# Borders of a 3x3 convolution stage: first norm by channel slot, part of the last group's statistics on ScalarE, merge on GpSimd, and four products of the last 1x1 convolution placed ahead of its scale

## The chip, the cores and the metric

The kernel runs on one core of one Trainium2 chip. The metric is the device time of one execution in microseconds (us). The engines are TensorE (PE, with its weight loads PEld), VectorE (DVE), ScalarE (ACT), GpSimd (POOL) and SyncE (SP, which here only issues DMAs).

## The reference

Two bottleneck blocks run one after the other on x of shape 64 x 1024 x 14 x 14, all in float32. A batch norm takes mean and variance over all 64 images and all pixels of a channel, from the very tensor that it normalizes.

```python
def _bn(x, gamma, beta):
    mean = jnp.mean(x, axis=(0, 2, 3), keepdims=True)
    var = jnp.var(x, axis=(0, 2, 3), keepdims=True)
    return gamma * (x - mean) * jax.lax.rsqrt(var + EPS) + beta

def block(x, ...):                                   # twice, with its own weights
    out = relu(_bn(conv1x1(x, w1) + b1, g1, be1))    # 1024 -> 256
    out = relu(_bn(conv3x3(out, w2) + b2, g2, be2))  # 256 -> 256, padding 1
    out = _bn(conv1x1(out, w3) + b3, g3, be3)        # 256 -> 1024
    return relu(x + softplus(residual_scale) * out)
```

## The kernel before

The 256 middle channels lie on 128 partitions in two slots, s = 0 and 1; the 1024 outer channels lie in eight. The images are taken two at a time as 32 tiles of 392 pixels for the 1x1 convolutions, and eight at a time as eight groups of 1568 pixels for the 3x3 convolution. The middle tensor of all images stays on the chip in `y_all`.

The order of the stages is: conv1 of block 0 (lines 1187 to 1207); conv2 of block 0 (`conv2`, line 543); a Gram matrix of its output, from which the statistics of conv3 are computed without conv3 (`gram`, line 904, and `conv3_stats`, line 981); then conv3 and the residual of block 0 together with conv1 of block 1 (`fused`, line 1060); conv2 of block 1; the Gram matrix of block 1; conv3 and the residual of block 1 (`residual`, line 1017, for the first and last tile, and `final`, line 1034, for pairs of tiles between). Between conv1 and conv2, and between conv2 and the Gram matrix, a batch norm closes: nothing of the next stage can start before the last value of the one before has entered the statistics. `aggregate` (line 1106) joins the partial statistics of each slot, and `affine` (line 1113) makes scale and shift from them by a chain of small instructions, one of them a square root on ScalarE.

Conv2 works by transforms along rows and columns. For each group `combine` (line 576) makes three pairs of row combinations, (1, 2), (3, 4) and (5, 0), in tiles t1, t2, ra and rb, with `stt` (line 574, VectorE) and `last` (line 571, ScalarE, the last row alone). `ready` (line 581) adds sums, differences and column differences, and has the filters loaded by SP, first the part ua and then the part ub (line 609). `Products` then multiplies on TensorE: `columns` goes into the banks even and odd, `whole` into l and m, and `biased` (line 679) moves these from PSUM on ScalarE. For the very first item the matmuls in `columns` are sorted so that slot 0 comes first (line 720). `finish` (line 751) is a generator on VectorE that turns the products of a group back into rows of `y_grp`.

The norm of the first conv happens in place: for group 0 before the first item (lines 854 to 855 and the function that `combine` calls between the two slots, line 860), for each later group on ScalarE while the group before is worked on (`long_work`, line 863). Group 0 is normalized so: slot 0 by ScalarE, rows 0 to 7 of slot 1 by VectorE, and the rest of slot 1 by ScalarE.

The statistics of conv2's output come in three ways. Group 0: bn_stats on VectorE (`first_stats`; `stat`, line 758, in five parts). Groups 1 to 6: two ScalarE passes for each slot with an accumulator, of value and of square around group 0's mean (`moment`, line 833). Group 7: bn_stats on VectorE in five parts. `merge` (line 839) joins the moments with small VectorE instructions and `entry` (line 818) writes them as one more bn_stats record.

In block 1 the statistics of conv3 end with 48 one-column matmuls into the bank ax; two products of the first tile, `made`, are computed ahead of them, into the two cx banks. `affine` follows, and `residual` computes the other six products, each with its own bank, and adds them to x.

Each engine works through its own list in order. The order within a list is partly that of the code (matmuls, `act`, and others wrapped in `keep_in_program_order`) and is otherwise set by a scheduler when the kernel is built. SP issues its DMAs in order, and a load waits until its buffer is free.

Of the kernel before, what the change touches and what calls it, by code (L numbers as in the profile page):

```python
# [41 lines left out]
P = 128  # L42
# [28 lines left out]

PARTS = 5

# [18 lines left out]
def bottlenecks(ctx: ExitStack, tc: tile.TileContext, x, w1s, w2s, w3s, pars, out):  # L92
# [450 lines left out]
    def conv2(psum, pool, b, par, aff, stats):  # L543
# [12 lines left out]
        moments = small.tile([P, MS, 2, NG - 2], FP, tag="moments", name="moments")  # L556
# [19 lines left out]
        def combine(g, pair, between=None):  # L576
# [40 lines left out]
            if pair[0] == 1:  # L617
                t1, t2 = new("t"), new("t")
                slots = [both] if between is None else [slice(s, s + 1) for s in range(MS)]
                for part in slots:  # L620
                    if part.start:
                        between()
                    last(t1, g, 2, -3.0, part)
                    last(t2, g, 1, -3.0, part)
                    for s in range(part.start, part.stop):
                        stt(t1[:, s, :full], rows(g, s, 2, 0, full), -4.0, rows(g, s, 4, 0, full))
                        stt(t2[:, s, :full], rows(g, s, 1, 0, full), -4.0, rows(g, s, 3, 0, full))
                    nc.vector.tensor_add(ra[:, part], t1[:, part], t2[:, part])
# [26 lines left out]
        class Products:  # L655
# [50 lines left out]
            def columns(self, *qs):  # L706

                r = self.r
                if self.four:
                    parts = {ODD: [(0, WH, D3M1, r[:, :, :, WH:])], EVEN: [(0, WH, D0M2, r[:, :, :, :WH])]}  # L710
                else:
                    parts = {
                        ODD: [(0, WH, D1, r[:, :, :, WH:]), (0, WH - 1, D3, r[:, :, :, WH + 1 :])],
                        EVEN: [(0, WH, D2, r[:, :, :, :WH]), (1, WH, D0, r[:, :, :, : WH - 1])],
                    }
                steps = [(q, o, part, s) for q in qs for o in range(MS) for part in parts[q] for s in range(MS)]
                if self.first:


                    steps.sort(key=lambda step: step[3])  # L720
                opened = set()
                for q, o, (a, e, k, v), s in steps:
                    to = self.banks[q][:, o].rearrange("p (l c) -> p l c", c=WH)[:, :, a:e]
                    matmul(
                        to, self.filter(s, o, k), v[:, s], start=self.first and q not in opened, stop=True,
                        skip_group_check=True,
                    )
                    opened.add(q)
                if self.first:
                    self.later(0, self.sums, ALU.add)  # L730
# [20 lines left out]
        def finish():  # L751


            for g in range(NG):
# [3 lines left out]
                def stat(k, lines):  # L758
                    if to is not None:
                        for o in range(MS):  # L760
                            nc.vector.bn_stats(to[:, o, k, :], lines[:, o])
# [25 lines left out]
                stat(2, out_rows[2])  # L787

# [7 lines left out]
                if g == NG - 1:  # L796
                    merge()
# [20 lines left out]
        def entry(half, count, mean, var):  # L818

            to = stats[:, :, 0, 3 * half : 3 * half + 3]  # L820
            nc.vector.memset(to[:, :, 0], float(count))
            nc.vector.tensor_copy(to[:, :, 1], mean)
            nc.vector.tensor_scalar(to[:, :, 2], var, float(count), None, ALU.mult)

        def begin():
# [5 lines left out]
            entry(0, GPX, mv[:, :, 0], mv[:, :, 1])  # L831

        def moment(g, o, k):
            act(
                idle, y_all[:, o, g * GPX : (g + 1) * GPX], (AF.Identity, AF.Square)[k], bias=center[:, o : o + 1],
                accum_out=moments[:, o, k, g - 1 : g],
            )

        def merge():

            n = GPX * (NG - 2)
# [3 lines left out]
            nc.vector.tensor_scalar(m, m, 1.0 / n, None, ALU.mult)  # L845
            var = small.tile([P, MS], FP, tag="m12var", name="m12var")
            nc.vector.tensor_mul(var, m[:, :, 0], m[:, :, 0])
            nc.vector.tensor_sub(var, m[:, :, 1], var)
            nc.vector.tensor_sub(m[:, :, 0], m[:, :, 0], center)
            entry(1, n, m[:, :, 0], var)  # L850


        top = 8
        norm(0, y_grp[:, 0, 0], aff)
        norm_vector(1, y_grp[:, 1, 0, :top], aff)

        def items():
            for g, pair in pairs:
                first = (g, pair) == pairs[0]
                for item in combine(g, pair, partial(norm, 1, y_grp[:, 1, 0, top:], aff) if first else None):  # L860
                    yield item

        def long_work(g, k):
# [6 lines left out]
            if g > 1 and i < 4:  # L870
                moment(g - 1, i // 2, i % 2)
# [241 lines left out]
    def affine(mv, n, par, g, be, conv_bias=None):  # L1113
# [10 lines left out]

        nc.vector.tensor_mul(q, r, v)
        nc.vector.scalar_tensor_tensor(q, q, -0.5, r, ALU.mult, ALU.mult)
        nc.vector.scalar_tensor_tensor(r, q, 1.5, r, ALU.add, ALU.mult)
        scale, shift = tl("scale"), tl("shift")
        nc.vector.tensor_mul(scale, r, par[:, g : g + n])
# [79 lines left out]
    for b in range(2):  # L1209
# [4 lines left out]
        aff = affine(aggregate(stats1, T - 3 + b), MS, pb, G1, BE1)  # L1214
        stats2 = keep.tile([P, MS, 1 + PARTS, nc.vector.BN_STATS_DIM], FP, tag="stats2", name=f"stats2_{b}")
# [3 lines left out]
        with tc.tile_pool(name=f"last_{b}", bufs=1) as one, tc.tile_pool(  # L1219
# [6 lines left out]
            with ExitStack() as scope:  # L1226
# [4 lines left out]
                with tc.tile_pool(name=f"gram_{b}", bufs=1) as pool:  # L1231
# [22 lines left out]
                    conv3_stats(psum, pool, grams, w3, mv3, ("cy", "cp", "cy", "cp" if b else "cx"))  # L1254
                aff = affine(mv3, CS, pb, G3, BE3, conv_bias=B3)
# [50 lines left out]
```

## Time and profile before

| what | us |
|---|---|
| median of 3 runs | 2015.49 (2012.01 to 2016.28) |
| the profiled execution | 2014.53 |
| its span, first to last instruction | 2012.5 |
| conv1 of block 0 | 0 to 308 |
| conv2 of block 0, to the scale of its norm | 308 to 604 |
| Gram matrix and conv3 statistics, block 0 | 604 to 700 |
| conv3 of block 0 with conv1 of block 1 | 700 to 1300 |
| conv2 of block 1, to the scale of its norm | 1300 to 1597 |
| Gram matrix and conv3 statistics, block 1 | 1597 to 1693 |
| residual of block 1 | 1693 to 2012.5 |

Times are counted from the first instruction. In a timeline a line has the start, the length from the first start to the last end of the instructions merged in it, the engine, the source line, the operation, what it writes and reads, and the number of instructions; in square brackets stands how long the engine was idle before, and who released it. In the chain of waits a line has start, share of time in us, and what was running. L169 is the helper through which all matmuls go, L327 the one for most of ScalarE's work, L574 is `stt`. In the table by stretches of time the columns are the length, then the busy time of PE, PEld, DVE, ACT and POOL with instruction counts, then the granted TensorE clock, the busy share of the DMA engines and GB/s.

### The profile page before, as it was taken

The numbers are of one execution on the slowest core, as the hardware profiler recorded it, in microseconds if no ns is written. First come the engines' busy times: TensorE is split into PE (matmuls) and PEld (weight loads), VectorE is DVE, ScalarE is ACT, GpSimd is POOL, SyncE is SP. The second block draws the span as 40 slices with busy tenths as digits, with TensorE's granted clock in tenths as the row PEclk, the third lists the DMA queues.
The fourth block names the chain that finished last, engine by engine and source line by source line (L and its number), as shares of the span: only waits on it lengthen the run. The fifth ranks groups of instructions, "written<-read, shape, count | busy, mean of one in ns | idle before, by whom it ended". The sixth has DMA issues, their size and how long they took to land.

```text
span 2012.5 us, 27547 instructions
## 1 busy us (share of the span) xinstructions
PE 1947.0 (97%) x9560; PEld 1640.9 (82%) x9560; DVE 1586.7 (79%) x2844; ACT 941.2 (47%) x1915; POOL 617.1 (31%) x676
## 2 busy tenths in 40 slices
PE   8999999999987999999999999899999888999999
PEld 4555558999987889999999999899999876555554
DVE  5788758999986566777777677699999864899997
ACT  1222214466645055555555555445566521555555
POOL 0111101121213133333433333211221140666665
PEclk9999999999998999999999999999999898999999
DMA  7866625555546534444444444256656374699998
GB/s 269 291 249 246 250 97 171 185 190 188 190 133 181 201 128 161 186 168 176 177 163 190 161 178 175 104 172 191 195 181 196 98 200 177 256 324 333 339 337 297
DMA packets 176218, 407.63 MB, mean 203 GB/s; under 512 B 12368, under 2 KB 143504, under 8 KB 159568
## 3 DMA queue, kind: packets, MB, share of 16 engines
q1 hardware_dynamic: 162208, 330.44, 48.0%
q10 hardware_dynamic: 5328, 50.86, 6.1%
q0 software_dynamic: 8544, 24.59, 3.6%
q8 instruction: 75, 1.23, 0.2%
q14 instruction: 63, 0.52, 0.1%
HBM read 267.95 MB, written 115.87 MB: 191 GB/s over the span
## 4 chain that ended last, share of the span: by engine, by line
PE 80%; DVE 12%; DMA 5%; ACT 1%; issue 1%; POOL 1%; SPq 0%; DVEq 0%; ACTq 0%; POOLq 0%
PE ay L169 16%; PE cy L169 13%; PE cp L169 11%; PE ap L169 10%; PE even L169 6%; PE odd L169 6%; PE m L169 5%; PE ax L169 5%; PE l L169 4%; PE cx L169 4%; DMA x<-mid 3%; DVE x L453 2%; PE ps L169 1%; DMA out<-x 1%; DVE sums L589 1%
## 5 line engine op out<-in xcount | busy, mean ns | idle before, releaser
L327 ACT ACTIVATE cu<-cy,scale 128x196 f32<-128x196 f32 (+1 forms) x552 | 257.3, 475 | 296.9 <-PE cy L169 289.4
L592 POOL TENSOR_TENSOR diffs<-r 128x448 f32<-128x448 f32 (+1 forms) x80 | 112.3, 1415 | 509.2 <-DVE r L574 262.7
L327 ACT ACTIVATE x<-x,shift 128x392 f32<-128x392 f32 x368 | 211.7, 614 | 69.3 <-POOL x L479 53.1
L453 DVE SCALAR_TENSOR_TENSOR x<-cp,scale,x 128x196 f32<-128x196 f32 (+1 forms) x368 | 178.0, 484 | 83.1 <-PE cp L169 81.0
L169 PE MATMUL cy<-ct,ws 128*128 128x196 f32 (+1 forms) x736 | 221.7, 383 | 2.5 <-ACT cu L327 2.5
L474 POOL TENSOR_TENSOR x<-x,cu 128x196 f32<-128x196 f32 (+1 forms) x184 | 167.5, 910 | 170.8 <-ACT cu L327 170.5
L169 PE MATMUL ay<-at,ws 128*128 128x196 f32 (+1 forms) x752 | 209.3, 381 | 1.0 <-ACT au L327 1.0
L479 POOL TENSOR_TENSOR x<-x,cu 128x392 f32<-128x392 f32 x124 | 126.1, 1017 | 190.9 <-DVE x L453 186.2
L169 PEld LDWEIGHTS ay<-at,ws 128*128 128x128 f32 x752 | 136.3, 190 | 35.1 <-ACT au L327 1.9
L169 PEld LDWEIGHTS cy<-ct,ws 128*128 128x128 f32 x736 | 133.6, 190 | 36.9 <-ACT cu L327 3.8
L500 POOL TENSOR_TENSOR x<-x,cu 128x392 f32<-128x392 f32 x120 | 125.1, 1043 | 83.5 <-DVE x L453 78.1
L169 PE MATMUL m<-sums,ua 128*128 128x224 f32 (+1 forms) x752 | 145.5, 336 | 0.0
L169 PE MATMUL cp<-zt 128*128 128x257 f32 x392 | 122.5, 395 | 16.3 <-DVE zt L948 16.3
L169 PE MATMUL cx<-y,w 128*128 128x196 f32 (+1 forms) x412 | 129.7, 402 | 5.0 <-DVE x L1025 5.0
L169 PEld LDWEIGHTS m<-sums,ua 128*128 128x128 f32 x752 | 131.3, 189 | 0.2
L453 DVE SCALAR_TENSOR_TENSOR x<-cx,scale,x 128x196 f32<-128x196 f32 (+1 forms) x184 | 89.1, 484 | 51.1 <-PE cx L169 50.8
L169 PE MATMUL cy<-y,w 128*128 128x196 f32 (+1 forms) x404 | 125.3, 396 | 0.0
L169 PE MATMUL even<-v,ub 128*128 128x224 f32 (+1 forms) x640 | 123.8, 334 | 0.7 <-ACT even L686 0.7
L169 PE MATMUL odd<-v,ub 128*128 128x224 f32 (+1 forms) x640 | 123.8, 335 | 0.2
L169 PE MATMUL l<-diffs,ub 128*128 128x224 f32 (+1 forms) x640 | 122.0, 333 | 0.0
L327 ACT ACTIVATE au<-ay 128x196 f32<-128x196 f32 (+1 forms) x141 | 53.8, 381 | 139.7 <-PE ay L169 139.0
L169 PE MATMUL cp<-y,ws 128*128 128x196 f32 (+1 forms) x368 | 113.8, 391 | 3.3 <-DVE x L453 1.8
(211 smaller groups left out, 4340.5 us busy)
## 6 DMA issues: line engine op xcount, KB each, us to landing
x<-in_x SPq DMA_DIRECT2D x62, 1568.0 KB, 6.7
ub<-u SPq DMA_DIRECT2D x80, 768.0 KB, 4.8
x<-mid SPq DMA_DIRECT2D x32, 1568.0 KB, 9.9
mid<-x ACTq DMA_DIRECT2D x31, 1568.0 KB, 5.2
out<-x SPq DMA_DIRECT2D x124, 392.0 KB, 6.6
ua<-u SPq DMA_DIRECT2D x96, 256.0 KB, 3.1
ub<-u SPq DMA_DIRECT2D x16, 1024.0 KB, 6.4
u<-y POOLq DMA_DIRECT2D x40, 256.0 KB, 6.3
```

What stands on the lines that cost most here:

```text
L169: tc.keep_in_program_order(nc.tensor.matmul(*args, **kw))
L327: tc.keep_in_program_order(nc.scalar.activation(*args, **kw))
L453: nc.vector.scalar_tensor_tensor(v, bank, self.scale[:, o : o + 1], v, ALU.mult, ALU.add)
L474: nc.gpsimd.tensor_add(self.part(1, 1), self.part(1, 1), u3)
L479: nc.gpsimd.tensor_add(v, v, self.u12)
L500: nc.gpsimd.tensor_add(v, v, self.u12[:, i * self.n : (i + 1) * self.n])
L589: nc.vector.tensor_add(sums, r[:, :, :, WH:], r[:, :, :, :WH])
L592: nc.gpsimd.tensor_sub(diffs, r[:, :, :, :WH], r[:, :, :, WH:])
```

## The change

Four things are edited.

First, the start of conv2. Scale and shift are made slot by slot, slot 1 first (`affine_by_slot`). Group 0 is normalized slot by slot just ahead of its combination: rows 7 to 13 by ScalarE and rows 0 to 6 by VectorE, for each slot. The matmuls of the first item take slot 1 first.

Second, the end of conv2. Of the five parts of group 7's statistics, VectorE keeps parts 3, 4 and 0. Parts 1 and 2, six rows of 112 pixels for each slot, are taken by ScalarE as two moments for each slot. The small instructions of the merge, behind its two reductions, run on GpSimd.

Third, in `affine` the multiplication by gamma is moved into r, ahead of the last step, so that the last step writes the scale.

Fourth, in block 1 four more products of the first tile, o = 2 to 5, are computed behind the conv3 statistics and ahead of the affine, into the banks cy and cp. Six of eight are then made ahead.

```diff
+LAST_PARTS = 3, 4, 0
...
-        moments = small.tile([P, MS, 2, NG - 2], FP, tag="moments", name="moments")
+        moments = small.tile([P, MS, 2, NG - 1], FP, tag="moments", name="moments")
...
-        def combine(g, pair, between=None):
+        def combine(g, pair, before=None):
...
-                slots = [both] if between is None else [slice(s, s + 1) for s in range(MS)]
+                slots = [both] if before is None else [slice(s, s + 1) for s in reversed(range(MS))]
                 for part in slots:
-                    if part.start:
-                        between()
+                    if before is not None:
+                        before(part.start)
...
-                    steps.sort(key=lambda step: step[3])
+                    steps.sort(key=lambda step: -step[3])
...
                 def stat(k, lines):
-                    if to is not None:
+                    if to is first_stats or to is not None and k in LAST_PARTS:
                         for o in range(MS):
-                            nc.vector.bn_stats(to[:, o, k, :], lines[:, o])
+                            nc.vector.bn_stats(to[:, o, k if to is first_stats else LAST_PARTS.index(k), :], lines[:, o])
...
                 stat(2, out_rows[2])
+                if g == NG - 1:
+                    for o in range(MS):
+                        lines = y_grp[:, o, g, 1 : 1 + 4 * full].rearrange("p (r k) l -> p r k l", k=4)[:, :, :2]
+                        for k in range(2):
+                            moment(lines, idle[:, : 2 * full * LINE].rearrange("p (r k l) -> p r k l", k=2, l=LINE), o, k, g)
+                    merge()
...
                 stat(4, end)
-                if g == NG - 1:
-                    merge()
...
-        def entry(half, count, mean, var):
+        def entry(eng, half, count, mean, var):
 
             to = stats[:, :, 0, 3 * half : 3 * half + 3]
-            nc.vector.memset(to[:, :, 0], float(count))
-            nc.vector.tensor_copy(to[:, :, 1], mean)
-            nc.vector.tensor_scalar(to[:, :, 2], var, float(count), None, ALU.mult)
+            eng.memset(to[:, :, 0], float(count))
+            eng.tensor_copy(to[:, :, 1], mean)
+            eng.tensor_scalar(to[:, :, 2], var, float(count), None, ALU.mult)
...
         def merge():
 
-            n = GPX * (NG - 2)
+            n = GPX * (NG - 2) + 2 * full * LINE
             m = small.tile([P, MS, 2], FP, tag="m12", name="m12")
             for o in range(MS):
                 nc.vector.tensor_reduce(m[:, o], moments[:, o], mybir.AxisListType.X, ALU.add)
-            nc.vector.tensor_scalar(m, m, 1.0 / n, None, ALU.mult)
+            eng = nc.gpsimd
+            eng.tensor_scalar(m, m, 1.0 / n, None, ALU.mult)
             var = small.tile([P, MS], FP, tag="m12var", name="m12var")
-            nc.vector.tensor_mul(var, m[:, :, 0], m[:, :, 0])
-            nc.vector.tensor_sub(var, m[:, :, 1], var)
-            nc.vector.tensor_sub(m[:, :, 0], m[:, :, 0], center)
-            entry(1, n, m[:, :, 0], var)
-
-
-        top = 8
-        norm(0, y_grp[:, 0, 0], aff)
-        norm_vector(1, y_grp[:, 1, 0, :top], aff)
+            eng.tensor_tensor(var, m[:, :, 0], m[:, :, 0], ALU.mult)
+            eng.tensor_sub(var, m[:, :, 1], var)
+            eng.tensor_sub(m[:, :, 0], m[:, :, 0], center)
+            entry(eng, 1, n, m[:, :, 0], var)
+
+        def first_norm(s):
+
+            top = 7
+            norm(s, y_grp[:, s, 0, top:], aff)
+            norm_vector(s, y_grp[:, s, 0, :top], aff)
 
         def items():
             for g, pair in pairs:
-                first = (g, pair) == pairs[0]
-                for item in combine(g, pair, partial(norm, 1, y_grp[:, 1, 0, top:], aff) if first else None):
-                    yield item
+                yield from combine(g, pair, first_norm if (g, pair) == pairs[0] else None)
...
+    def affine_by_slot(stats, first, par, g, be, order):
+
+        both = [small.tile([P, MS], FP, tag=f"by_slot_{n}", name=n) for n in ("scale", "shift")]
+        for s in order:
+            mv = aggregate(stats[:, s : s + 1], first)
+            affine(mv, 1, par, g + s, be + s, to=[v[:, s : s + 1] for v in both])
+        return both
+
-    def affine(mv, n, par, g, be, conv_bias=None):
+    def affine(mv, n, par, g, be, conv_bias=None, to=None):
...
+        scale, shift = to or (tl("scale"), tl("shift"))
         nc.vector.tensor_mul(q, r, v)
         nc.vector.scalar_tensor_tensor(q, q, -0.5, r, ALU.mult, ALU.mult)
-        nc.vector.scalar_tensor_tensor(r, q, 1.5, r, ALU.add, ALU.mult)
-        scale, shift = tl("scale"), tl("shift")
-        nc.vector.tensor_mul(scale, r, par[:, g : g + n])
+        nc.vector.tensor_mul(r, r, par[:, g : g + n])
+        nc.vector.scalar_tensor_tensor(scale, q, 1.5, r, ALU.add, ALU.mult)
...
-        aff = affine(aggregate(stats1, T - 3 + b), MS, pb, G1, BE1)
-        stats2 = keep.tile([P, MS, 1 + PARTS, nc.vector.BN_STATS_DIM], FP, tag="stats2", name=f"stats2_{b}")
+
+        aff = affine_by_slot(stats1, T - 3 + b, pb, G1, BE1, (1, 0))
+        stats2 = keep.tile([P, MS, 1 + len(LAST_PARTS), nc.vector.BN_STATS_DIM], FP, tag="stats2", name=f"stats2_{b}")
...
                     conv3_stats(psum, pool, grams, w3, mv3, ("cy", "cp", "cy", "cp" if b else "cx"))
+                if b == 1:
+                    made += [conv3(psum, 0, o, w3, tag) for o, tag in zip(range(2, 6), ("cy", "cp") * 2)]
                 aff = affine(mv3, CS, pb, G3, BE3, conv_bias=B3)
```

More of the change, by code (lines that the diff above doesn't have):

```diff
@@ L830, in begin, with moment @@
             nc.vector.tensor_scalar(center, mv[:, :, 0], -1.0, None, ALU.mult)
-            entry(0, GPX, mv[:, :, 0], mv[:, :, 1])
-        def moment(g, o, k):
-            act(
-                idle, y_all[:, o, g * GPX : (g + 1) * GPX], (AF.Identity, AF.Square)[k], bias=center[:, o : o + 1],
-                accum_out=moments[:, o, k, g - 1 : g],
+            entry(nc.vector, 0, GPX, mv[:, :, 0], mv[:, :, 1])
+        def moment(y, to, o, k, g):
+            act(
+                to, y, (AF.Identity, AF.Square)[k], bias=center[:, o : o + 1], accum_out=moments[:, o, k, g - 1 : g],
             )
         def merge():
-            n = GPX * (NG - 2)
+            n = GPX * (NG - 2) + 2 * full * LINE
             m = small.tile([P, MS, 2], FP, tag="m12", name="m12")
@@ L870, in long_work @@
             if g > 1 and i < 4:
-                moment(g - 1, i // 2, i % 2)
+                o = i // 2
+                moment(y_all[:, o, (g - 1) * GPX : g * GPX], idle, o, i % 2, g - 1)
         made, finished = items(), finish()
```

## The prediction

> **What bounds the kernel now.** I read the page first: engines, then the rows of slices.
>
> ```profile
> PE 1947.0 (97%) x9560; PEld 1640.9 (82%) x9560; DVE 1586.7 (79%) x2844; ACT 941.2 (47%) x1915; POOL 617.1 (31%) x676
> PEclk9999999999998999999999999999999898999999
> ```
>
> PE is busy for 97% of the span, so time can be won only where it stands still or runs at a lower clock. That is at the borders of the stages, the slices under 9. The change touches three kinds: the start of conv2 (twice), its end (twice), and the gap ahead of the last residual of block 1. For each I read the timeline, and the chain of waits for what ended last.
>
> Start of conv2, block 1 (timeline; the last line is the list of DMA issues of that window, with the median time to landing):
>
> ```profile
> 1300.15 0.42 DVE L378 SCALAR_TENSOR_TENSOR y<-ap,par,au 128x196 f32<-128x196 f32 x1
> 1301.35 0.62 SPq L609 DMA_DIRECT2D ub<-u  x1
> 1306.20 0.62 DVE L628 TENSOR_TENSOR r<-t 128x448 f32<-128x448 f32 x1
> 1308.10 3.11 PE L169 MATMUL even<-r,ub 128*128 128x224 f32 x8 [4.12 <-DVE r L628]
> ub<-u SPq DMA_DIRECT2D x1, 1024.0 KB, 6.4
> ```
>
> The first product needs slot 0's r, written at 1306.82, and the filters ub, issued at 1301.35 and landed 6.4 us later, near 1307.75. The wait is put down to DVE r, but the r meant was long done: the filters came last. Block 0 agrees by its chain, where slot 0's r (313.88 + 0.62 = 314.50) and the filters tie:
>
> ```profile
> 309.08 5.45 DMA ub<-u
> 314.66 3.11 PE even L169 x8
> ```
>
> End of conv2, block 0 (timeline):
>
> ```profile
> 593.13 1.73 DVE L761 BATCH_NORM_STATS2 stats<-y 128x6 f32<-128x336 f32 x4
> 596.57 1.70 PE L169 MATMUL odd<-v,ub 128*128 128x224 f32 x8
> 602.39 0.29 ACT L1121 ACTIVATE sd<-mv,eps 128x2 f32<-128x2 f32 x1 [6.61 <-DVE mv L1110]
> 605.23 1.30 PE L936 MATMUL cy<-ident,y 128*128 128x128 f32 x4 [6.96 <-DVE y L1233]
> ```
>
> PE is done at 598.27; DVE works without a pause from 589 to the last statistics at 601.5, then aggregates and makes the norm's scale. PE stands 6.96. So DVE's tail is the path.
>
> Gap in block 1 (timeline):
>
> ```profile
> 1693.12 0.17 DVE L1012 COPY mv<-ax 128x16 f32<-128x16 f32 x1 [3.83 <-PE ax L169]
> 1697.30 1.15 DVE L1025 SCALAR_TENSOR_TENSOR x<-cx,scale,x 128x392 f32<-128x392 f32 x2
> 1698.06 2.95 PE L169 MATMUL cx<-y,w 128*128 128x392 f32 x4 [4.98 <-DVE x L1025]
> ```
>
> Two conv3 products are ready; the third waits 4.98 for a bank that the first add frees, and that add waits for the affine.
>
> **The change, part by part.**
>
> *Start of conv2, slot by slot.* In block 0 slot 1's statistics are complete at 306.21 (305.64 + 0.57), 1.4 us before slot 0's last result is begun (L378, 307.65). On DVE the order now is: aggregate slot 1, v, then L378, which waits for PE until 307.63; the rest of slot 1's affine queues behind it. From 308.28 some ten short steps of 0.08 to 0.2 with the two statistics between (0.57, 0.24) bring the shift at 309.9; then half a norm (784 elements by the 896 row: 0.66 + 0.56), two t of 0.42 and r 0.54: slot 1's r at about 313.0, instead of slot 0's at 314.5. The second r comes at about 315.6, as now (315.65). Added: 8 short DVE steps (0.6) and 672 more elements of norm on DVE (1.1), against 0.8 less on ACT. But SP's order and waits are unchanged: ub is issued when L378 is done, which does not move, and lands at 314.53 and about 1307.75. Gain: 0. The second slot is asked for only after 16 matmuls (3.11 + 2.77), so it is not late. Bounds: were ub no limit, 1.5 per block gained; the 1.7 of added DVE work is hidden by the 1.6 that DVE idles in 330 to 340 (8.39 busy of 10.00), and without that cover costs up to 1.7 per block, since the chain runs on DVE from 341 to 407. I take 0, as these cancel.
>
> *End of conv2.* DVE loses four bn_stats (593.13 to 594.78: 1.65) and six short steps of the merge (0.07 + 0.06 + 0.07 + 0.07 + 0.08 + 0.07 = 0.42 in the chain). It keeps the two reductions, now behind ACT. ACT gets four moments over 672 elements: by the row of 1568 (1.60 each) and that of a 672 norm (0.93), 0.85 each. They start when slot 0's rows are written (590.8), interleaved with the two bank copies (0.44 each), and end at 595.1. The copy of odd comes at 594.25 instead of 593.16; PE asks for it at 596.57. Next in ACT's queue is the copy ls, due at 595.24. DVE reaches the first reduction at 593.05 (its moments: 592.5) and the second at 595.2 (595.1): about no wait. Some results are now used directly after they are made: +0.15. Net 1.65 + 0.42 - 0.15 = 1.9. Aggregation over 24 values instead of 36: 0.07. The affine's reorder takes one of the dependent steps (0.195) to an independent one (0.08): 0.11. Sum 2.1 per block, 4.2 in all.
>
> On POOL six short instructions, five of them waiting for the one before, follow the second reduction (595.4); the aggregation needs them at 599.6, slack 4.2. Nothing but six memsets is queued behind. The trace has no such instruction: nearest are a memset of 128x2 (0.10) and a tensor_tensor of 128x196 (0.78), so 0.6 to 4.7: 0 to 0.5 late. By the Trainium skill ("GPSIMD Engine Reference", 3.1) GpSimd takes about twice VectorE's time for a two-input operation; with DVE's 0.15 that is an estimate of 0.3, or 1.8 for six: not late, taken. Its section 2.1 speaks against the change: the first call of a freshly loaded GpSimd kernel costs about 6 us. No tensor_scalar or copy ran there before. The row: the first diffs of the trace took 1.34, under the mean of its kind. By the row 0; by the rule up to 12 once.
>
> *Gap in block 1.* Four more products are put behind the ax products, at 1693.10. In block 0, where PE does run on, this line has the same shape:
>
> ```profile
> 700.25 2.96 PE L169 MATMUL cx<-y,w 128*128 128x392 f32 x4
> ```
>
> By its chain 2.82, then 1.35, 1.38, 1.32. Before, six products took 2.95 + 2.49 + 4 x 1.32 = 10.73 from 1698.06, to 1708.79. After, from 1693.10: 2.82 + 5 x 1.33 = 9.5, to 1702.6, gain 6.2; if two are slow as before, 10.73, to 1703.8, gain 5.0. I take 5.8. Adds on DVE start at 1697.2 and take 0.54: six done by 1700.5, the last two follow PE; banks for products seven and eight are free by 1699. ACT's relus (0.6) keep up. The final stage moves up as a whole: its first five x tiles were issued from 1663.0 on and DMA is at 0.19 and 0.35 in 1680 to 1720; later loads wait for outputs, which move too.
>
> *The clock.* What speaks against adding this up:
>
> ```profile
> 624.65:628.07 3.42, 0.29 (x1) 0.29 (x2) 2.86 (x4) 3.42 (x3) 0.00 (x0) 0.50 0.88 237
> 628.07:631.48 3.41, 3.41 (x11) 2.84 (x11) 3.41 (x6) 2.62 (x2) 0.00 (x0) 0.50 0.27 65
> 631.48:634.90 3.42, 3.42 (x23) 3.14 (x22) 3.42 (x7) 0.00 (x0) 1.07 (x3) 1.00 0.02 6
> ```
>
> (Stretches 3.41 long; PE's busy time comes first, the third number from the end is the granted clock.) After a pause PE has half its clock to the end of the first full stretch. The Trainium skill ("TensorE: Matmul & The Clock Gate", Part 1) gives a free-running window of about 3.4 us that does not start with the kernel. So if PE resumes 2 us earlier inside the same window, the extra time runs at half speed, and only 1 arrives. By this execution's grid block 0's 2.1 would shrink to about 1; by the rule the grid lies elsewhere in each run, and in the mean all of it arrives. I sum the whole and put up to 1.7 per restart into the range.
>
> *Sum.* 0 + 4.2 + 5.8 = 10.0. The profiled execution took 2014.53 (span 2012.5, 2.0 around it): 2004.5. The median of the runs shown, 2015.49, is 1.0 above it: 2005.5.
>
> **Rivals.**
> 1. More: the windows fall well, or slot 1's earlier start relieves DVE. For it: PE's first 16 matmuls of conv2 run at 0.50 for 6 us; against: ub. 10 + 4: 2001.5.
> 2. The end's gain is eaten, by the clock as above, or by 1.7 more DVE work where DVE is the path (341 to 407). 5.8 + 0.7 = 6.5: 2009.0.
> 3. The final stage is bound by transfers (DMA 0.88 to 0.99 from 1740 on), and the 5.8 are given back. Against it: PE is busy 19.86 of 20 there, and DMA starts the stage idle. 4.2: 2011.3.
> 4. Slower: GpSimd's merge takes the place of DVE's. It costs beyond 4.2 for the six, and turns the sign beyond 4.2 + 5.0 = 9.2 in each block, 1.5 an instruction. With two slow starts of 6 in each: 1.8 + 12 - 4.2 = 9.6 late, twice, less 10: 2024.7. Against: the rows of 0.10 and 1.34.
>
> **How the numbers follow.** Likeliest 0.61 (2005.5, own range 2002.5 to 2008.5), rival 1 0.12, rival 2 0.16, rival 3 0.08, rival 4 0.03. A measurement of this kernel tells about 0.2%, 4 us: 2011.5 and 2019.5. Faster: 0.61 + 0.12 + 0.14 + half of rival 3, 0.91; slower 0.03; the same 0.06. The range for 8 in 10 runs from the middle of rival 1 to beyond rival 2: 2001.0 to 2010.5.
>
> **What would show it.** First matmul of conv2 still at the landing of ub, r of slot 1 over a micro-second ahead of it. From PE's last conv2 product to sd 2.1 less than 4.1, four moments near 0.85, POOL's six done before DVE's last statistics. No pause of PE behind ax in block 1, the eighth product 9.5 to 10.7 behind the ax products instead of 15.7, and from there to the end 303.7, as now. Wrong: an aggregation that waits for POOL, a conv2 start that moves, or x loads that PE waits for.

## The result, and the profile after

| | before | after |
|---|---|---|
| median, us | 2015.88 (2012.01 to 2019.83, 4 runs) | 2006.01 (2004.56 to 2007.74, 4 runs) |
| ratio | 1 | 0.9951, 95% interval 0.993 to 0.9972 |
| profiled execution, us | 2014.53 | 2004.56 |
| its mean granted TensorE clock | 0.984 | 0.987 |

The forecast was 2005.5. Line numbers after are higher than before: all matmuls go through L171, `stt` is L576, group 7's bn_stats is L763, the merge L849 to L855.

The start of conv2 in block 0 (timeline; conv1's last result, the issue of the ub filters on SP, slot 1's r, the first products):

```profile
308.07 0.63 DVE L380 SCALAR_TENSOR_TENSOR y<-ap,par,au 128x392 f32<-128x392 f32 x1 [0.98 <-PE ap L171]
309.51 0.57 SPq L611 DMA_DIRECT2D ub<-u  x1
312.96 0.63 DVE L630 TENSOR_TENSOR r<-t 128x448 f32<-128x448 f32 x1
315.85 3.11 PE L171 MATMUL even<-r,ub 128*128 128x224 f32 x8 [3.74 <-DVE t L576]
```

Slot 1's r is complete 5.51 after y has begun. The first product begins 7.77 after y, so 2.3 later than its r. The bracket names a t of VectorE, which was done long before; what PE lacked was ub: it was issued at 309.51, and the median from issue to landing of this transfer is 6.2 in this profile, which gives about 315.7. In another execution of the same kernel, further below, the bracket says so.

The end of conv2 in block 0 (timeline; a ScalarE moment, the second reduction, GpSimd's first and last instruction, PE's last product, the last statistics, the square root, the Gram matrix's first work on PE):

```profile
591.85 0.86 ACT L329 ACTIVATE idle<-y,center 128x672 f32<-128x672 f32 x1 [1.17 <-DVE y L576]
...
596.41 0.17 DVE L849 TENSOR_REDUCE m<-moments 128x2 f32<-128x14 f32 x1 [0.18 <-ACT idle L329]
596.67 0.28 POOL L851 TENSOR_SCALAR m<-m 128x4 f32<-128x4 f32 x1 [18.53 <-DVE m L849]
597.79 0.18 POOL L828 COPY stats<-m 128x2 f32<-128x2 f32 x1
597.55 1.69 PE L171 MATMUL odd<-v,ub 128*128 128x224 f32 x8
600.23 1.14 DVE L763 BATCH_NORM_STATS2 stats<-y 128x6 f32<-128x448 f32 x2
601.75 0.30 ACT L1135 ACTIVATE sd<-mv,eps 128x2 f32<-128x2 f32 x1 [4.95 <-DVE mv L1116]
604.59 1.30 PE L942 MATMUL cy<-ident,y 128*128 128x128 f32 x4 [5.35 <-DVE y L1248]
```

From PE's last product (599.24) to sd it is 2.51; before it was 4.13. GpSimd is done at 597.97, over 3 us before DVE aggregates (601.29). DVE waits 0.18 for the second reduction's moment. PE stands 5.35 instead of 6.96.

The gap in block 1 (timeline):

```profile
1688.51 1.93 PE L171 MATMUL ax<-ones,q 128*128 128x1 f32 x16
1690.29 2.86 PE L171 MATMUL cy<-y,w 128*128 128x392 f32 x4
1690.47 0.17 DVE L1018 COPY mv<-ax 128x16 f32<-128x16 f32 x1 [3.84 <-PE ax L171]
...
1700.17 0.63 DVE L1031 SCALAR_TENSOR_TENSOR x<-cy,scale,x 128x392 f32<-128x392 f32 x1 [0.69 <-PE cy L171]
```

The four new products follow the one-column products at once; the 4.98 of before is gone. The last line is the eighth add, 9.70 after mv; before it came 15.69 after mv.

Cut at the same marks, the two profiled executions differ so (us, block 0 / block 1; "y" is conv1's last result, "sd" the start of the square root on ScalarE, "ready" the start of PE's first product behind the second and longer pause of the Gram stage, in block 0 of before at 627.78 after 8.19 idle; "mv" the copy out of ax):

| stretch | before | after |
|---|---|---|
| y to first product of conv2 | 7.01 / 7.95 | 7.77 / 7.63 |
| first to last product of conv2 | 283.60 / 283.54 | 283.40 / 282.46 |
| last product to sd | 4.13 / 4.13 | 2.51 / 2.51 |
| sd to ready | 25.39 / 25.29 | 25.87 / 25.30 |
| ready to mv | 72.65 / 72.06 | 72.87 / 72.11 |
| mv to the eighth add (block 1) | 15.69 | 9.70 |
| eighth add to the end (block 1) | 303.68 | 302.61 |

### The profile page after: what moved, and what is told of

It reads as the page before. It is cut to its first block, busy times and chain, and to the rows that moved or that the text cites. A ratio compares the mean times of both kernels' runs of the same rounds, so it can differ in the third digit from the quotient of the medians.

```text
span 2002.8 us, 27581 instructions
## 1 busy us (share of the span) xinstructions
PE 1945.9 (97%) x9560; PEld 1640.7 (82%) x9560; DVE 1586.3 (79%) x2842; ACT 948.3 (47%) x1933; POOL 618.5 (31%) x690
## 4 chain that ended last, share of the span: by engine, by line
PE 79%; DVE 13%; DMA 4%; ACT 1%; issue 1%; POOL 1%; SPq 1%; DVEq 0%; ACTq 0%
PE ay L171 16%; PE cy L171 13%; PE cp L171 11%; PE ap L171 10%; PE odd L171 5%; PE even L171 5%; PE ax L171 5%; PE m L171 5%; PE l L171 4%; PE cx L171 4%; DMA x<-mid 2%; DVE x L455 2%; DVE sums L591 1%; PE ps L171 1%; DMA out<-x 1%
## 5 line engine op out<-in xcount | busy, mean ns | idle before, releaser
L171 PE MATMUL cy<-ct,ws 128*128 128x196 f32 (+1 forms) x736 | 222.0, 383 | 2.5 <-ACT cu L329 2.5
L171 PE MATMUL ay<-at,ws 128*128 128x196 f32 (+1 forms) x752 | 209.4, 382 | 1.0 <-ACT au L329 1.0
L171 PEld LDWEIGHTS ay<-at,ws 128*128 128x128 f32 x752 | 136.4, 190 | 35.0 <-ACT au L329 2.0
L171 PEld LDWEIGHTS cy<-ct,ws 128*128 128x128 f32 x736 | 133.7, 190 | 36.9 <-ACT cu L329 3.8
L171 PE MATMUL m<-sums,ua 128*128 128x224 f32 (+1 forms) x752 | 145.5, 336 | 0.0
L171 PE MATMUL cp<-zt 128*128 128x257 f32 x392 | 123.0, 396 | 16.2 <-DVE zt L954 16.2
L171 PEld LDWEIGHTS m<-sums,ua 128*128 128x128 f32 x752 | 131.4, 190 | 0.2
L171 PE MATMUL cy<-y,w 128*128 128x196 f32 (+1 forms) x404 | 126.0, 398 | 0.0
L171 PE MATMUL cx<-y,w 128*128 128x196 f32 (+1 forms) x404 | 125.2, 396 | 0.0
L171 PE MATMUL even<-v,ub 128*128 128x224 f32 (+1 forms) x640 | 123.8, 335 | 0.7 <-ACT even L688 0.7
L171 PE MATMUL odd<-v,ub 128*128 128x224 f32 (+1 forms) x640 | 123.9, 335 | 0.2
L171 PE MATMUL l<-diffs,ub 128*128 128x224 f32 (+1 forms) x640 | 122.0, 334 | 0.0
L171 PE MATMUL cp<-y,ws 128*128 128x196 f32 (+1 forms) x368 | 113.9, 391 | 2.5 <-DVE x L455 1.0
```

Source lines behind the costliest of these rows:

```text
L171: tc.keep_in_program_order(nc.tensor.matmul(*args, **kw))
```

## The experiments

The theory at this point: the gap gives what the trace shows, the end gives 1.6 per block, the start nothing, because ub bounds it. The rivals: the end's gain does not arrive, because the half clock or VectorE takes it; the start carries part of the gain.

### One part at a time

The four products alone, on the kernel before:

```diff
                 conv3_stats(psum, pool, grams, w3, mv3, ("cy", "cp", "cy", "cp" if b else "cx"))
+            if b == 1:
+                made += [conv3(psum, 0, o, w3, tag) for o, tag in zip(range(2, 6), ("cy", "cp") * 2)]
             aff = affine(mv3, CS, pb, G3, BE3, conv_bias=B3)
```

> The kernel before, with only the four more conv3 products behind the ax products of block 1. My theory: PE's pause of 4.98 us there goes, the eighth product's add begins 9.7 us after the copy out of ax (it was 15.7), and the stage behind keeps its length, so the whole run is 6 us (0.3%) shorter. Rival (the final stage is bound by transfers): the add still comes 9.7 us after the copy, but from there to the end it takes up to 6 us longer and the run is as long as before.

Measured: 2009.0 against 2016.04, ratio 0.9967 (0.9955 to 0.9979). Its trace has 9.62 from mv to the eighth add, 6.1 less than before. The medians differ by 7.0; the interval of the ratio makes that 4.2 to 9.1, so the time is not told apart from the 6.1 between the two marks.

The end of conv2 alone (the changed kernel with the start, the affine and the gap of before):

```diff
-    steps.sort(key=lambda step: -step[3])
+    steps.sort(key=lambda step: step[3])
...
-        aff = affine_by_slot(stats1, T - 3 + b, pb, G1, BE1, (1, 0))
+        aff = affine(aggregate(stats1, T - 3 + b), MS, pb, G1, BE1)
...
-                    made += [conv3(psum, 0, o, w3, tag) for o, tag in zip(range(2, 6), ("cy", "cp") * 2)]
```

> The kernel before, with only the end of conv2 changed: parts 1 and 2 of group 7's statistics on ScalarE, the merge on GpSimd; the affine as before. My theory: from PE's last product of conv2 to the square root it takes 2.5 us instead of 4.1 in both blocks, 1.6 us less each, 3.2 us in the mean of many runs, but in any one run the clock windows let between 0 and 5 us arrive. Rival (GpSimd's merge ends last): the aggregation waits for POOL and the 4.1 stays. Rival (the whole 10 us of the change comes from here and not from the gap): 8 us or more shorter.

Measured: 2014.69, ratio 0.999 (0.998 to 1.0), with a wide spread, 2007.13 to 2017.43. The trace has 2.50 from the last product to sd in both blocks, so 3.2 less in all; the median moved by 1.3, and the interval, 0 to 4.0, holds both 3.2 and nothing.

The start by slot alone, with the reordered affine:

```diff
+        aff = affine_by_slot(stats1, T - 3 + b, pb, G1, BE1, (1, 0))
...
+        def first_norm(s):
+            top = 7
+            norm(s, y_grp[:, s, 0, top:], aff)
+            norm_vector(s, y_grp[:, s, 0, :top], aff)
```

> The kernel before, with only the start of conv2 by slot, slot 1 first, and the affine's new order of steps. My theory: the first product of conv2 still waits for the filters ub, 7.0 to 8.0 us after the last result of conv1 begins, although slot 1's r is written 2 us earlier than that; the run is within 2 us of before. Rival (the slot order pays): the first product starts 1 us or more earlier after the last result and the run is 2 to 4 us shorter. Rival (the added work on VectorE, which is the path in the first group, costs): 2 to 3.5 us longer.

Measured: 2015.28, ratio 0.9997 (0.9989 to 1.0006). Nothing, as forecast. The profiles agree: from y to the last product of conv2 it is 290.1 to 292.4 in the ten blocks of the five profiles with the start by slot (mean 290.9), and 289.2 to 292.4 in those of the five without it (mean 290.6); the runs with ub in halves or PE kept busy, below, are left out. The reordered affine, which this kernel has too, gave nothing either: its steps lie behind sd, and from sd to the first work of the Gram stage it is 2.84 in every profile, with the new order and with the old.

### Is it ub that bounds the start, and is an earlier start worth anything?

The changed kernel, with the ub filters of the first item fetched in two halves, slot 1's first:

```diff
-   nc.sync.dma_start(out=v.rearrange(...), in_=us[b][i][:, :, :, a:e].rearrange(...))
+   first = g == 0 and i == order[0][0] and a
+   for s in (slice(1, 2), slice(0, 1)) if first else (slice(0, MS),):
+       nc.sync.dma_start(out=v[:, s].rearrange(...), in_=us[b][i][:, s, :, a:e].rearrange(...))
```

> The changed kernel, with ub of the first item of each conv2 loaded in two halves, that of slot 1 first, so that the first 16 matmuls need only half a megabyte. My theory (ub bounds the start): the first product starts when slot 1's r is there, 5.6 us after the last result of conv1 begins instead of 7.7, about 2 us earlier in each block; of these 4 us between 0 and 4 arrive at the end, as VectorE is the path later in the first group. Rival (something else holds the first product, such as r of the second slot): the first product starts no earlier.

Measured: 2011.58, 0.9975 of before (0.9964 to 0.9985). That is 4.5 less than before, where the changed kernel had 9.9 less (8.2 in a second set of runs, below): the halves on top of the change lose 3.8 to 5.4, although the first product does come earlier, 5.73 and 5.78 after y. The time is lost later. The timeline of PE in this run:

```profile
313.22 0.95 PE L171 MATMUL even<-r,ub 128*128 128x224 f32 x4 [1.70 <-DMA ub<-u]
...
353.87 4.45 PE L171 MATMUL even<-r,ub 128*128 128x224 f32 x14 [2.73 <-ACT even L688]
```

ScalarE, which PE waited for, had itself been waiting (its timeline in the same run):

```profile
352.94 0.88 ACT L688 ACTIVATE even<-m,par 128x224 f32<-128x224 f32 x2 [5.79 <-DVE f L743]
```

And VectorE was working without a pause. The table by stretches, first of this run, then of the changed kernel (length, then busy PE, PEld, DVE, ACT, POOL with counts, granted clock, DMA share, GB/s):

```profile
350.00:355.00 5.00, 2.27 (x11) 1.83 (x11) 5.00 (x10) 1.60 (x4) 0.00 (x0) 0.95 0.54 175
355.00:360.00 5.00, 5.00 (x21) 4.86 (x20) 5.00 (x11) 0.00 (x0) 0.00 (x0) 0.71 0.03 12
```

```profile
350.00:355.00 5.00, 5.00 (x28) 4.96 (x27) 5.00 (x11) 1.03 (x3) 0.00 (x0) 1.00 0.66 219
355.00:360.00 5.00, 5.00 (x29) 4.95 (x28) 5.00 (x11) 1.11 (x3) 0.00 (x0) 1.00 0.53 154
```

DVE's column reads 5.00 of 5.00 in all four rows. A PE that starts 2 us earlier comes 2 us earlier to a place where it depends on VectorE, stands there for 2.73, and pays on top: the clock is at half from 354.5 to 357.9. From the first to the last product it is 286.48 and 286.26, 3.1 and 3.8 more than in the changed kernel, so that the last product comes 1.0 and 2.0 later after y than there. So ub bounds the first product, but VectorE bounds what it is worth. In this profile 1.4 more is lost from mv to the eighth add (11.07 for 9.70), at another half clock.

The same halves on the kernel before, slot 0's first, as a control:

> The kernel before, with the ub filters of the first item of each conv2 fetched in two halves, slot 0's first: the control for the run with halves on top of the change. Its first product can start at slot 0's r, 6.85 after y, instead of 7.0 to 9.1. If VectorE sets the pace soon after (340 to 365), this is worth nothing: 2015 to 2017, and TensorE pauses near 350 for what it is ahead. If ub's landing is the limit, 1 to 2 per block: 2012 to 2014. If the smaller transfers themselves make the later filters late, it is slower by 4 to 6, as the run on top of the change was against it: 2020 to 2022.

Measured: 2015.22 against 2017.27, ratio 0.999 (0.9983 to 0.9996), and 282.25 and 282.36 from first to last product. From the first product to 400 us PE's longest wait is 0.20. Halved transfers do no harm by themselves; by the interval they gain 0.8 to 3.4. Here the products start at 6.95 and 6.98, as slot 0's r allows. The loss in the run above has two parts that these runs do not separate in time: the start is earlier still, and the start by slot gives VectorE more to do. The second shows in the traces. The step of VectorE on which ScalarE waits there (f, L743 above) ends 45.4 and 45.2 after y with halves and the start by slot, no earlier than in the best blocks of the changed kernel without halves (45.2), but 44.3 and 44.5 in the control. So the start by slot moves the place that sets the pace by 0.9 to the later side, and the earlier ub of that run did not make it good.

From the other side, PE was kept busy in its wait for ub, on the changed kernel. The products repeated here read one column of `ident` over and over and are 448 columns wide; they are called one-column products in the expectation, but are not of the kind 128x1 that comes below:

```diff
-        for tag in COLUMNS * 2:
+        for tag in COLUMNS * 4:
```

> The whole change, and four more of the one-column products (results unused) that already stand at the start of each conv2, so that TensorE runs for about 3 us more of its wait for the ub filters. If the half clock of the first 7 us of conv2 costs what it seems to (first to last product 283.4 and 282.5 instead of 281.5), each block gains 1 to 1.5: 2003 to 2004. If VectorE sets the pace from 340 to 365 us (busy 5.00 of every 5 there), TensorE only comes to wait there, and the time stays at 2006. If one-column products count as idle for the clock, the granted clock stays at 0.5 from about 315 to 321 as now, and the time at 2006.

Measured: 2008.25 (2005.57 to 2010.38), not better than the changed kernel. The half clock at the start is gone from the trace (granted 1.00 from 314 to 323, where the changed kernel has 0.5 from 314.8 to 321.7). Part of what PE wins there it waits for later:

```profile
354.44 3.13 PE L171 MATMUL even<-r,ub 128*128 128x224 f32 x16 [0.96 <-ACT even L686]
```

In block 1 the wait at this place is 0.22. That fits the theory of VectorE's pace; the expected 1 to 1.5 per block did not come in the time.

### The start taken out, and the merge moved back

The whole change without the start by slot:

```diff
-        aff = affine_by_slot(stats1, T - 3 + b, pb, G1, BE1, (1, 0))
+        aff = affine(aggregate(stats1, T - 3 + b), MS, pb, G1, BE1)
...
-            top = 7
-            norm(s, y_grp[:, s, 0, top:], aff)
-            norm_vector(s, y_grp[:, s, 0, :top], aff)
+        top = 8
+        norm(0, y_grp[:, 0, 0], aff)
+        norm_vector(1, y_grp[:, 1, 0, :top], aff)
```

> The whole change without the start by slot (first norm, combination and affine as before): four more conv3 products and the statistics split. If the parts add up and the start is worth nothing, this equals the whole change: 2006.0, and PE's last product of conv2 to sd is 2.5, first moment of mv to the seventh add 9.7. If the start gives something only together with the rest, it is slower than the whole change by that: 2007 to 2009. If the added VectorE work of the start costs (14 rows of the first norm there instead of 8, some eight short steps more), it is faster: 2003 to 2005.

Measured: 2011.12 against 2017.27, ratio 0.9965 (0.9954 to 0.9976). (The "seventh add" in this expectation is the eighth of the tables here.)

The whole change with the merge on VectorE:

```diff
-            eng = nc.gpsimd
+            eng = nc.vector
```

> The whole change with the six instructions of the merge on VectorE instead of GpSimd. If GpSimd takes them off the path, the time from PE's last conv2 product to sd grows from 2.51 by six VectorE steps of 0.07 (the rows of before), to 2.9, and the total by 0.8, to 2006.8. If the hand-over between the engines costs as much as it saves, it stays at 2.5 and 2006.0.

Measured: 2004.21, ratio 0.9938 (0.9926 to 0.995). The tail grew as the first theory says, to 2.93 and 2.92: GpSimd takes 0.42 per block off the path, the six steps of 0.07. But the median fell, and the median of the version without the start had risen by 5. No trace has a cause of that size in the edits, so something else of several microseconds varies between executions.

### What varies: where the half clock falls

In the run without the start, the stretch from ready to mv, whose code is untouched, took 75.80 and 75.14 instead of 72.87 and 72.11. The cause is in the one-column products, which last 8.0 and 8.1 there for 5.4. The changed kernel shows the same from execution to execution. PE's timeline in a second set of the changed kernel, the same file as the first, in block 1:

```profile
1685.05 1.02 PE L171 MATMUL cp<-w,g 128*128 128x512 f32 x2
1685.91 4.45 PE L171 MATMUL ax<-g,w 128*128 128x1 f32 x32
1690.22 3.55 PE L171 MATMUL ax<-ones,q 128*128 128x1 f32 x16
```

In the first set:

```profile
1684.16 1.02 PE L171 MATMUL cp<-w,g 128*128 128x512 f32 x2
1685.02 3.63 PE L171 MATMUL ax<-g,w 128*128 128x1 f32 x32
1688.51 1.93 PE L171 MATMUL ax<-ones,q 128*128 128x1 f32 x16
```

The 48 one-column products last 7.9 instead of 5.4. The half-clock periods of each profile begin and end on a grid of 3.41. The stretches on that grid, again the second set and then the first:

```profile
1685.05:1688.46 3.41, 3.41 (x27) 2.93 (x25) 1.88 (x3) 0.00 (x0) 0.00 (x0) 1.00 0.00 0
1688.46:1691.87 3.41, 3.41 (x18) 3.41 (x18) 0.00 (x0) 0.00 (x0) 0.00 (x0) 0.51 0.02 5
1691.87:1695.29 3.42, 3.42 (x12) 2.79 (x13) 1.48 (x8) 0.07 (x1) 0.00 (x0) 0.50 0.00 0
```

```profile
1683.58:1686.99 3.41, 3.41 (x23) 2.54 (x21) 2.46 (x4) 0.00 (x0) 0.00 (x0) 1.00 0.00 0
1686.99:1690.40 3.41, 3.41 (x32) 3.41 (x33) 0.00 (x0) 0.00 (x0) 0.00 (x0) 1.00 0.02 5
1690.40:1693.81 3.41, 3.41 (x7) 1.81 (x7) 3.31 (x15) 0.30 (x1) 0.00 (x0) 0.50 0.00 0
```

PE counts as busy throughout, and still the clock falls. In the first row of the second set, only the 0.86 before 1685.91 are wide products and the rest is one column wide: the next stretch is at half. In the first row of the first set it is 1.44 (to 1685.02): the next stretch keeps its clock, and only the one after it, behind a stretch of one-column products alone, is at half. Whether the one or the other happens hangs on where the grid lies, and it lies elsewhere in each execution. All fourteen profiles, with two such places each, agree: in the stretch in which the one-column products begin, up to 1.16 of wide products were followed at once by half clock (eight places, the 48 products then last 7.8 to 8.2), and 1.22 or more by one further stretch at full clock (twenty places, 5.4 to 6.9). Over all profiles ready to mv took 72.0 to 75.8 with the same code.

So versions were set side by side once more, on one chip: the changed kernel, the merge on VectorE, no start by slot, and a combination of all that had looked good (before's start, the gap, the split statistics with the merge on VectorE, ub in halves with slot 0 first).

> The changed kernel once more, unaltered, on the chip of the three runs beside it, since the versions have been timed on different chips (the kernel before had 2015.9, 2016.0 and 2017.3 there). If runs differ mainly by the half-clock windows that fall into them, the mean time follows the mean granted clock by 1.2 to 1.8 us per 0.001: near 2006 at 0.9865, 2008 to 2009 at 0.985.

> The changed kernel with the merge on VectorE, again, beside the changed kernel on the same chip. The trace gave it a longer tail at the end of conv2 (2.93 for 2.51 from the last product to sd), the time a lower median (2004.2 for 2006.0). If the tail is what it costs, it is slower by 0.8; if the earlier median was the chip's or the clock's, it is within 1.5 of the run beside it; if the merge on GpSimd costs elsewhere, it is faster by 1.5 or more again.

> The changed kernel without the start by slot, again, beside the changed kernel on the same chip. Its one measurement (2011.1 against 2017.3) was at a mean granted clock of 0.983, and its profile has 3 us more in the one-column products before mv in each block than the changed kernel's. If that is chance, it now equals the run beside it within 1.5; if the start by slot is worth something, it is slower by 2 or more again.

> Before's start, the four conv3 products and the split statistics with the merge on VectorE, and the ub filters of the first item in two halves, slot 0's first. Added up from the single runs: gap 7.0, the end 3.2 less 0.8, halves of ub 2.0 (2015.2 against 2017.3): 11.4 less than before, about 1.5 under the changed kernel. If the halves' 2.0 were chance of the clock, it equals the changed kernel within 1.

Measured, against 2015.81: 2007.57 (0.9958, 0.9943 to 0.9973), 2007.26 (0.9961, 0.9947 to 0.9976), 2008.56 (0.9964, 0.995 to 0.9978) and 2008.18 (0.996, 0.9946 to 0.9975). The intervals overlap, so the four are not told apart. The lead of the merge on VectorE and the lag of the version without the start did not come again, nor did the combination's 1.5. The changed kernel is not beaten.

In its second profile the start of conv2 ran at full clock, and the wait there carries its right name:

```profile
314.24 1.66 PE L171 MATMUL even<-r,ub 128*128 128x224 f32 x8 [3.05 <-DMA ub<-u]
```

First to last product took 283.19 in that block, against 283.40 with half a clock for 6.9 us: one more sign that PE does not set the pace there.

### The parts at one clock

Each execution has its mean granted clock beside its time. A straight line was fitted to all of them, with a level for each kernel and one common slope. The slope is 1.39 us less for 0.001 more clock, and a scatter of about 1.3 is left. The levels, read at a clock of 0.985, have standard errors of 0.2 (before) to 0.6:

| kernel | executions | mean us | mean clock | at 0.985 |
|---|---|---|---|---|
| before | 66 | 2016.5 | 0.9837 | 2014.6 |
| start alone | 14 | 2015.9 | 0.9846 | 2015.3 |
| end alone | 14 | 2013.5 | 0.9834 | 2011.3 |
| gap alone | 5 | 2009.2 | 0.9860 | 2010.6 |
| gap and end | 12 | 2009.4 | 0.9839 | 2007.9 |
| the whole change | 10 | 2006.6 | 0.9859 | 2007.9 |
| merge on VectorE | 12 | 2006.2 | 0.9862 | 2008.0 |
| the combination | 6 | 2007.5 | 0.9853 | 2008.0 |
| before, ub in halves | 21 | 2014.9 | 0.9840 | 2013.5 |
| the change, ub in halves | 7 | 2010.8 | 0.9863 | 2012.6 |
| the change, PE kept busy | 5 | 2008.2 | 0.9876 | 2011.8 |

At one clock the parts add up: the gap 4.0, the end 3.3 (the traces show 1.6 per block), the start -0.7, together 6.6, and the whole has 6.7. In plain means they do not: gap and end together are 2009.4, no less than the gap alone with 2009.2. That the end's gain arrives in the time is therefore argued from the fit; the traces show it only as a shorter path.

The fit gives the gap less than the 6.0 of the traces because it takes the clock out, and part of the 6.0 is clock. Before, the clock is at half through PE's pause of 4.98 and behind it, to 1703.3; in the changed kernel's first profile it is back at 1693.8. The last of three such stretches in before, and the one behind the half clock in the changed kernel:

```profile
1699.80:1703.20 3.40, 3.40 (x6) 1.72 (x6) 0.62 (x1) 0.62 (x1) 0.00 (x0) 0.50 0.00 0
```

```profile
1693.81:1697.23 3.42, 3.42 (x11) 1.99 (x11) 3.32 (x11) 1.93 (x4) 0.00 (x0) 1.00 0.00 0
```

Half clock for 6.83 less is 0.0017 of the mean clock of the span, which at 1.39 makes an estimate of 2.4, and 4.0 + 2.4 is about 6. This part is not sure to come. At this place the clock is at half for 10.24 in all four profiles without the four products; in the ten with them it is 3.41 in four, 6.83 in one, and 10.24 in the five in which the one-column products had already lost the clock. From ready to the eighth add, the profiles without the four products have 87.4 to 88.0; the first four have 81.6 to 81.9, the one 83.1, and the five 85.4 to 85.8. What it takes without the four products when the one-column products of block 1 lose the clock, no profile shows. The version with gap and end has a mean clock of 0.9839, no more than before.

The slope is one price for all places, and it does not hold everywhere: the run with PE kept busy in its wait has the highest clock, 0.9876, and gained no time by it, so that its level at one clock lies 3.9 above the changed kernel's.

## Why the prediction was right, point by point

The time, 2006.0 and in the second set 2007.6, lies by 2005.5 and within its own range of 2002.5 to 2008.5. Each set is known to some 3 or 4 us only (5.6 to 14.1 and 5.4 to 11.5 less than before), so that it came within 0.5 is luck. By its steps:

- *Start of conv2: 0.* Right, and for the stated reason as far as the first product goes: ub landed after slot 1's r, by 2.3 instead of 1.5. The prediction took the 1.7 of added VectorE work as hidden and an early ub as worth 1.5. Both were off. With ub earlier the whole was 3.8 to 5.4 slower, since VectorE is busy 5.00 of 5.00 from 350 to 360 and PE then stands. And of the added VectorE work 0.9 is left at the step that sets the pace there, which a late ub hides. The rival with slot 1's earlier start as a relief for DVE had it the wrong way round.
- *End of conv2: 2.1 per block.* It was 1.62. Of the terms, the four bn_stats (1.65), six merge steps (0.42; the merge on VectorE showed 0.42) and the shorter aggregation (0.07) are as put. The second reduction waited 0.18 for about none, and what is left to the measured 1.62, about 0.3, is put down to the direct use of fresh results, which the prediction had at 0.15: 1.65 + 0.42 + 0.07 = 2.14, and 2.14 - 0.2 - 0.3 = 1.64. The affine's reorder, counted with 0.11, gave 0: the steps from 1/sd on follow each other at 0.2 in both orders. Why the step that was to become independent still takes 0.2 was not tested.
- *The GpSimd chain: 0 late.* Right. It took 1.30 against the estimate of 1.8, in steps of 0.18 to 0.28, and nothing like 6 us appeared at the first of them, which took 0.28. The Trainium skill's price for a first call of a freshly loaded kernel ("GPSIMD Engine Reference", section 2.1) did not apply to these instructions. The slower rival falls with it.
- *The gap: 5.8.* The first trace shows 6.0 (15.69 to 9.70), inside 5.0 to 6.2, and the time of the gap alone, 7.0 with an interval of 4.2 to 9.1, does not contradict it. The clock was in this sum: it counted two slow products before, and one (6.2) or two (5.0) after. What it did not see is that the one-column products ahead of the gap can lose the clock first: in the ten profiles with the four products mv to the eighth add is 9.57 to 11.07, and in five of them the loss ahead of mv comes on top.
- *The final stage moves as a whole.* Right: 303.7 before, 302.6 to 304.4 in all runs. The rival of transfers falls.
- *The clock.* Right that the grid lies elsewhere in each run; that in the mean the end's gain arrives holds at one clock, by the fit, and is not shown by the plain times. But the restarts it named matter little: behind conv2, sd to ready is 25.3 to 26.1 in all runs, however many half-clock stretches there are. The place that matters, the one-column products ahead of mv, was not seen.

So the sum of 10.0 had the right mechanism in its two large parts, with the end 1.0 too high: the traces give 3.2 + 6.0 = 9.2, where 4.2 + 5.8 was put. The times, 9.9 and 8.2 less than before, cannot tell 9.2 from 10.0.

## What to carry to other kernels

A transfer that bounds the first instruction of a stage need not bound the stage: look some tens of microseconds further for an engine that is busy in the whole of every stretch before paying for an earlier start. A pause of TensorE can cost its length and a half clock behind it, so filling one with work that is needed anyway can give more than the pause: here 6.0 in the first trace for a pause of 4.98. And where a kernel's time varies with the granted clock, compare versions on one chip, with the clock beside each time, and keep in mind that the edit itself can change the clock; medians of six runs here put two versions 7 us apart that a second set had 1.3 apart.

## What was not expected of the hardware

TensorE's clock falls while the engine is counted busy. In the stretch 1688.46 to 1691.87 PE is busy 3.41 of 3.41 at a granted 0.51, behind a stretch with 0.86 us of wide products and the rest one column wide; with 1.44 us of wide products in the stretch the clock stayed at 1.00 for one more. Over 28 such places the border lay between 1.16 and 1.22. The 48 one-column products then take 7.8 to 8.2 instead of 5.4 and more. The Trainium skill ("TensorE: Matmul & The Clock Gate", Part 1) speaks of how busy the engine has been in a free-running window; the window, 3.41, agrees with these rows, but busy in the profile's sense cannot be what is counted here.

GpSimd's small instructions were short: 0.18 to 0.28 on 128x2 and 128x4, where VectorE has 0.14 to 0.17 in the run with the merge on it. The profile's spans on GpSimd are rough, but from the start of the first to the end of the sixth it is 1.30.
